# Decoder layer, feed-forward: when the finished rows of the first two blocks are stored

## The chip, the cores and the metric

The kernel runs on one core of one Trainium2 chip. The metric is the device time of one launch in microseconds (us). TensorE (PE) multiplies matrices, with its weight loads shown apart (PEld); VectorE (DVE), ScalarE (ACT) and GpSimd (POOL) work on elements; SyncE (SP) issues transfers (DMAs), which 16 DMA engines carry out. SP and POOL issue through different hardware queues, q1 and q0 in the profile.

## The reference, cut to what matters

`x` is (8, 256, 512) in float32, 2048 tokens of width 512. A layer has three parts, each followed by a residual sum and a layer norm:

```python
x = _layernorm(x + attention(x))
x = _layernorm(x + recurrence(x, ctx))
gate_w, up_w, down_w = three spline_reconstruct(...)      # 2048x512, 2048x512, 512x2048
gate, up = x @ gate_w.T, x @ up_w.T
x = _layernorm(x + (silu(gate) * up) @ down_w.T)
```

The three weights are cubic splines of few control points. The kernel uses that: it multiplies with parts of the weights exactly, and represents what is smooth by a few sums.

## The kernel before, in words

Attention and recurrence fill the first 400 us of the span; the change doesn't touch them. The feed-forward (from about 401 us) works in four blocks (`NG = 4`, loop variable `b`) of 512 tokens (`GT`), each four row tiles of 128 tokens (`TC = 4`). Everything is float32. Each engine's instructions run in the order in which the program writes them (the class `Ordered` sees to that; it is also why all lines of the profile read L308, so that tiles, not lines, tell the work apart). What isn't ready makes the engine or the queue wait, and all behind it too. A block has these steps:

1. **Inputs** (`inputs(b + 1)`, written in block b for b = 1 and 2; those of blocks 0 and 1 were made in the attention part). `tr_x2` transposes the rows of `x2`, `x2T` holds them in SBUF. They are written to a scratch tensor `xd` in device memory: four large transfers on POOL's queue, four tiny ones on SP's, three of them ahead of the block's gathers. Products `ps_mom` make moments, written to a scratch tensor `md` on POOL's queue. Then SP reads windows of `xd` (four transfers, 1408 KB) and moments from `md` (two, 640 KB) into `xg`, the operand of the next block's products. For blocks 2 and 3 these reads are kept in the list `reads` and issued by SP after the gathers of block b.
2. **Gate and up** (`gate_up(b, j)`, eight pairs). Four products `pg` and `pu`, Silu on ACT, a product on DVE into `inter`, two tiles a pair.
3. **Gathers** (`gather(b, t)`, sixteen). SP copies each `inter` tile, SBUF to SBUF, 256 KB, into every eighth partition of `nat`; eight tiles fill one `nat`, and there are two.
4. **Exact part** (`exact(b, t)`, sixteen steps of four products `y`). After the first step of block b the chains of `outcome(b - 1, t)` start (step 7).
5. **Sums** (`into_sums`, four times, after exact step 7). Products `ps_s` read `nat`: the first pair of each of the four reads all of the first `nat`, that is gathers 0 to 7, the second pair gathers 8 to 15. ACT or DVE evicts them, and POOL issues the transfer `fin<-sum` (256 KB), in this document a *fin*.
6. **Finish** (`finish`, in the last block `finish_apart`). After the last exact step the product `y<-fin` needs all four fins of the block.
7. **Outcome** (`outcome(b, t)`, a generator that a list of chains steps on). Transposes `tr_y`, residual sum and layer norm into `h3` (a tile of pool `rows`, which has 6 buffers), and as its last act the store of 128 x 512 values to `out`, 256 KB, issued by SP. It runs in the exact part of block b + 1, for the last block after `finish_apart`.

So SP's queue in blocks 1 and 2 is, in order: three small `xd` writes, 16 gathers, one small `xd` write, four window reads, two moment reads, and the four stores of the block before. Block 3 has 16 gathers, four stores of block 2 and at the end four of its own. PE's order is `tr_x`, the pairs (with `ps_mom` after the third), exact steps 0 to 7 with `tr_y` after the first, `ps_s`, exact steps 8 to 15, finish.

Of the kernel before, what the change touches and what calls it, by code (L numbers as in the profile page):

```python
# [17 lines left out]
P = 128  # L18
# [8 lines left out]
NG = NT // GT  # L27
# [288 lines left out]
def decoder_kernel(ctx: ExitStack, tc: tile.TileContext, x, xT, ctxT, wq, wkT, wvT, woT, wdownT, wup, decay, up_taps, down_taps, mom_f, sum_f, out, plan):  # L316
    nc = tc.nc
# [27 lines left out]
    nc = Ordered(tc)  # L345
    units, chains = [], []

    def slot():

        for c in list(chains):  # L350
            if next(c, c) is c:
                chains.remove(c)

    def fill(n):

        for i in range(n):
            if units:
                next(units[0][1])
                units[0][2] -= 1
                if not units[0][2]:  # L360
                    units.pop(0)
            if i % 2:
                slot()
                some_taps()

    def norm_plain(h, s, o, other=None):

        nm = small.tile([P, 1], F32, tag="nm", name="nm")
        nc.vector.tensor_scalar(nm, s, -1.0 / D, None, ALU.mult)
        yield  # L370
        ss = small.tile([P, 1], F32, tag="ss", name="ss")
        nc.scalar.activation(o if other is None else other, h, AF.Square, bias=nm, accum_out=ss)
        yield
        va = small.tile([P, 1], F32, tag="va", name="va")
        nc.gpsimd.tensor_scalar(va, ss, 1.0 / D, EPS, ALU.mult, ALU.add)
        rs = small.tile([P, 1], F32, tag="rs", name="rs")
        nc.gpsimd.tensor_tensor(rs, va, neghalf[:, 0:1], ALU.pow)
        yield
        nc.vector.tensor_scalar(o, h, nm, rs, ALU.add, ALU.mult)
# [457 lines left out]
    sf = work.tile([P, NTILE, K2], F32, name="sf", bufs=1)  # L837
    nc.sync.dma_start(out=sf, in_=sum_f)
    made[0] = -1e9
    inters, ys, sorted_, xps, nats = {}, {}, {}, {}, {}  # L840

    def gate_up(b, j):

        pgs, pus = [], []
        for w, pool, tag, to in ((wg, ps_mm, "mm", pgs), (wu, ps_big, "big", pus)):
            for h in range(2):
                at = slice(h * K2, (h + 1) * K2)
                ps = pool.tile([P, GT], F32, tag=tag, name="pg" if w is wg else "pu")
                nc.tensor.matmul(ps, lhsT=w[at, j * P : (j + 1) * P], rhs=xgs[b][at, j, :], start=True, stop=True)
                to.append(ps)  # L850
        for h in range(2):
            sg = work.tile([P, GT], F32, tag="sg", name="sg")
            nc.scalar.activation(sg, pgs[h], AF.Silu)
            inter = work.tile([P, GT], F32, tag="inter", name="inter", bufs=NTILE)
            nc.vector.tensor_tensor(inter, pus[h], sg, ALU.mult)
            inters[b, 2 * j + h] = inter

    def gather(b, t):

        g, r = t // NSUM, t % NSUM  # L860
        if not r:
            nats[b, g] = work.tile([P, NSUM, GT], F32, tag=f"nat{g}", name="nat", bufs=1)
        nc.sync.dma_start(out=nats[b, g][r::NSUM], in_=inters[b, t])

    def exact(b, t):

        if t == 0:
            ys[b] = [ps_big.tile([P, GT], F32, tag="big", name=f"y{d}") for d in range(ND)]
        for d in range(ND):
            q = slice(d * 32, (d + 1) * 32)  # L870
            nc.tensor.matmul(
                ys[b][d], lhsT=wd[q, t * P : (t + 1) * P], rhs=inters[b, t][q, :], start=(t == 0), stop=(b == NG - 1 and t == NTILE - 1)
            )

    def into_sums(b, v):

        if v == 0:
            sorted_[b] = late.tile([P, ND, GT], F32, tag="fin", name="fin")
        acc = ps_mm.tile([P, GT], F32, tag="mm", name="ps_s")
        for g in range(NTILE // NSUM):  # L880
            for a in range(2):
                u = 2 * v + a
                nc.tensor.matmul(
                    acc[a * K2 : (a + 1) * K2, :],
                    lhsT=sf[:, g * NSUM + u, :],
                    rhs=nats[b, g][:, u, :],
                    start=(g == 0),
                    stop=(g == NTILE // NSUM - 1),
                )
        o = work.tile([P, GT], F32, tag="inter", name="sum", bufs=NTILE)  # L890
        (nc.vector.tensor_copy if v % 2 else nc.scalar.copy)(o, acc)
        nc.gpsimd.dma_start(out=sorted_[b][v::ND], in_=o)
# [14 lines left out]
    def finish_apart(b):  # L907


        y = late.tile([P, ND, GT], F32, tag="ys", name="ys")  # L910
        for d in range(ND):
            (nc.vector.tensor_copy if d % 2 else nc.scalar.copy)(y[:, d, :], ys[b][d])
        ys[b] = y
        acc = [ps_mm.tile([P, GT], F32, tag="mm", name="ps_c") for _ in range(ND)]
        chain = [outcome(b, t, ps_big, "big") for t in range(TC)]
        for n, at in enumerate((slice(0, GT // 2), slice(GT // 2, GT))):
            for d in range(ND):
                nc.tensor.matmul(
                    acc[d][:, at],
                    lhsT=wd[:, (NTILE + d) * P : (NTILE + d + 1) * P],  # L920
                    rhs=sorted_[b][:, d, at],
                    start=True,
                    stop=True,
                )
                nc.vector.tensor_tensor(y[:, d, at], acc[d][:, at], y[:, d, at], ALU.add)
                if n and d == 1:
                    next(chain[0])
                    next(chain[1])
                    next(chain[0])
        next(chain[2])  # L930
        next(chain[3])
        chains.extend(chain)

    def outcome(b, t, pool=ps_mm, tag="mm"):

        tr = pool.tile([P, D], F32, tag=tag, name="tr_y")
        for d in range(ND):
            nc.tensor.transpose(tr[:, d * P : (d + 1) * P], ys[b][:, d, t * P : (t + 1) * P], ident)
        yield
        h3 = rows.tile([P, D], F32, tag="row", name="h3")  # L940
        s3 = small.tile([P, 1], F32, tag="s3", name="s3")
        nc.vector.scalar_tensor_tensor(h3, tr, 1.0, xps[b][:, t, :], ALU.mult, ALU.add, accum_out=s3)
        yield from norm_plain(h3, s3, h3, tr)
        r0 = (b * TC + t) * P
        nc.sync.dma_start(out=out[r0 : r0 + P, :], in_=h3)

    def residual(b):

        xp = late.tile([P, TC, D], F32, tag="x2p", name="x2p")
        xps[b] = xp  # L950
        i = 0
        for at, h0, n, dr, m in copies:
            for a in range(n):
                nc.gpsimd.tensor_copy(
                    xp[:, :, at + a * m : at + (a + 1) * m],
                    x2[:, b * TC : (b + 1) * TC, h0 + dr * a : h0 + dr * a + 26 * (m - 1) + 1 : 26],
                )
                i += 1
                if i % 6 == 0:
                    yield  # L960

    def settle():
        while chains:
            slot()

    for b in range(NG):
        if 0 < b < NG - 1:
            units.append(["i", inputs(b + 1), 2 * DC])
            fill(DC)
        for j in range(NTILE // 2):  # L970
            gate_up(b, j)
            gather(b, 2 * j)
            gather(b, 2 * j + 1)
            if b:
                slot()
            if b and j == 2:
                fill(DC)
        if b == 0:
            fill(2 * DC)
        while reads:  # L980
            reads.pop(0)()
        for t in range(NTILE):
            exact(b, t)
            if b and t == 0:
                chains += [outcome(b - 1, c) for c in range(TC)]
            slot()
            if b == 0 and t < 5:
                slot()
            if b == 0 and t == 4:
                settle()  # L990
                done.close()
                late = ffn["mom"] = ctx.enter_context(tc.tile_pool(name="late", bufs=1, side="right"))
            if t == 7:
                settle()
                chains.append(residual(b))
                for v in range(NSUM // 2):
                    into_sums(b, v)
        assert not units
        (finish if b + 1 < NG else finish_apart)(b)
# [53 lines left out]
```

## Time and profile before

| | us |
|---|---|
| median of three runs | 603.2 |
| the three runs | 602.25, 603.2, 605.68 |
| the profiled execution | 604.72 |
| its span, first to last instruction | 602.9 |

The difference of the last two, 1.8 us, lies around the span. In the profiled execution the granted TensorE clock averaged 0.994 of full speed. The feed-forward stretches of PE in it:

| block | pairs begin | sums `ps_s` | finish ends |
|---|---|---|---|
| 0 | 401.06 | 431.62 to 438.64 | 449.35 |
| 1 | 451.09 | 479.48 to 486.52 | 501.00 |
| 2 | 502.74 | 531.13 to 538.17 | 550.19 |
| 3 | 550.19 | 574.79 to 581.90 | 594.9 with the last `tr_y` |

How to read the profile: a line of a group gives line, engine, operation, `out<-in` by the program's tile names and the number of instructions. A chain of waits follows the work that ended last back to what released it. A windows view gives for each stretch the busy time of each engine (with its number of instructions), the granted clock, the busy share of the 16 DMA engines and what they moved in GB/s. SP's timeline shows when a transfer was issued, not when it landed; landings come from the trace's semaphore updates.

### The profile page before, as it was taken

To read this page: it belongs to the slowest core of one execution; us is meant where nothing else is said; L and a number is where in the kernel's file an instruction comes from. 1 tells how busy PE (TensorE), PEld (TensorE's weight loads), DVE (VectorE), ACT (ScalarE), POOL (GpSimd) and SP (SyncE) were. 2 spreads that over 40 slices of the span, in tenths; PEclk is the share of its full clock that TensorE was granted. 3 is DMA by queue.
4 is the path that set the end of the run, shared out by engine and by line. 5 is a ranking of instruction groups with operands and counts; after the bars stand their busy time and mean duration, and the time that the engine had idled before them with its cause. 6 is when DMAs were issued, how large, how long until landed. Compare 5 with 4: busy or idle time off the path is not lost.

```text
span 602.9 us, 9715 instructions
## 1 busy us (share of the span) xinstructions
PE 578.9 (96%) x3354; PEld 294.1 (49%) x3354; DVE 337.1 (56%) x750; ACT 277.9 (46%) x820; POOL 218.7 (36%) x495
## 2 busy tenths in 40 slices
PE   9999999998999999999999899999999989999994
PEld 4544555555455555555555555444343434433443
DVE  0203634658676665786664877766826505623716
ACT  0115644656654555664554677564315303513502
POOL 0001997165544335544340212200371261143144
PEclk9999999999999999999999999999999999999998
DMA  8104253034224115324110564669129975984941
GB/s 299 59 0 157 80 169 112 27 110 147 61 69 141 35 54 175 105 71 130 46 36 5 167 158 114 174 152 213 39 79 247 194 220 150 231 208 140 212 152 70
DMA packets 38960, 75.50 MB, mean 125 GB/s; under 512 B 3936, under 2 KB 8288, under 8 KB 38912
## 3 DMA queue, kind: packets, MB, share of 16 engines
q1 hardware_dynamic: 34576, 62.75, 39.4%
q0 software_dynamic: 3328, 10.96, 5.5%
q10 hardware_dynamic: 1008, 1.18, 0.6%
q8 instruction: 26, 0.43, 0.3%
q14 instruction: 22, 0.18, 0.1%
HBM read 42.86 MB, written 11.04 MB: 89 GB/s over the span
## 4 chain that ended last, share of the span: by engine, by line
PE 82%; DVE 9%; ACT 3%; DMA 3%; issue 2%; POOL 0%; POOLq 0%; DVEq 0%; ACTq 0%
PE y L308 10%; PE ps_k L308 9%; PE ps_v L308 9%; PE ps_o L308 8%; PE ps_q L308 7%; PE tr_e L308 7%; PE sc L308 5%; PE av L308 5%; PE pg L308 5%; PE ps_s L308 5%; PE pu L308 5%; DVE nmax L308 3%; DMA fin<-sum 3%; PE ps_mom L308 2%; ACT e L308 2%; DVE eT L308 2%
## 5 line engine op out<-in xcount | busy, mean ns | idle before, releaser
L308 ACT ACTIVATE e<-sc,nmax 128x256 f32<-128x256 f32 x256 | 120.3, 481 | 101.0 <-DVE nmax L308 100.9
L308 DVE TENSOR_REDUCE nmax<-sc 128x2 f32<-128x512 f32 x128 | 84.5, 682 | 73.6 <-PE sc L308 67.6
L308 POOL TENSOR_TENSOR taps<-taps 128x256 f32<-128x256 f32 (+1 forms) x144 | 88.9, 617 | 32.9 <-DMA taps<-in_down_taps 25.1
L308 PEld LDWEIGHTS tr_e<-ident,e 128*128 128x128 f32 x512 | 56.9, 140 | 25.2 <-issue 22.5
L308 PE MATMUL tr_e<-ident,e 128*128 128x128 f32 x512 | 68.3, 276 | 0.6 <-DVE eT L308 0.4
L308 PE MATMUL y<-inter,wd 32*128 32x512 f32 x512 | 63.0, 598 | 0.0
L308 PE MATMUL ps_o<-w_o,yT 128*128 128x512 f32 x128 | 60.0, 600 | 1.5 <-DVE eT L308 1.2
L308 PE MATMUL ps_k<-xT_g,w_k 128*128 128x512 f32 x128 | 58.7, 600 | 0.6 <-DVE eT L308 0.6
L308 PE MATMUL ps_v<-w_v,xT_g 128*128 128x512 f32 x128 | 58.6, 598 | 0.4 <-DVE eT L308 0.4
L308 PE MATMUL ps_q<-xT_g,w_q 128*128 128x512 f32 x128 | 58.2, 596 | 0.0
L308 POOL TENSOR_SCALAR va<-ss 128x1 f32<-128x1 f32 x32 | 7.3, 228 | 135.3 <-ACT x L308 85.8
L308 POOL TENSOR_TENSOR rs<-va,neghalf 128x1 f32<-128x1 f32 x48 | 28.8, 600 | 69.7 <-DVE va L308 66.9
L308 ACT ACTIVATION_READ_ACCUMULATOR e<-sc,nmax 128x1 f32 x256 | 53.3, 208 | 0.0
L308 DVE TENSOR_TENSOR inter<-pu,sg 128x512 f32<-128x512 f32 x64 | 41.3, 687 | 18.3 <-PE pu L308 9.4
L308 ACT ACTIVATE sg<-pg 128x512 f32<-128x512 f32 x64 | 37.3, 597 | 18.4 <-PE pg L308 18.4
L308 DVE COPY eT<-tr_e 128x512 f32<-128x512 f32 x64 | 43.7, 683 | 0.5 <-PE tr_e L308 0.4
L308 PEld LDWEIGHTS y<-inter,wd 32*128 32x128 f32 x512 | 26.7, 184 | 32.7 <-issue 26.9
L308 PE MATMUL av<-eT,v_g 128*32 128x256 f32 x512 | 36.7, 385 | 5.0 <-ACT eT L308 2.7
L308 ACT COPY eT<-tr_e 128x512 f32<-128x512 f32 x64 | 37.5, 586 | 2.4 <-PE tr_e L308 2.4
L308 POOL TENSOR_TENSOR r<-r 128x1024 f32<-128x1024 f32 x8 | 15.2, 1894 | 63.3 <-DMA r<-in_ctxT 63.2
L308 PE MATMUL sc<-k_g,q_g 32*128 32x256 f32 x512 | 37.4, 401 | 0.2 <-ACT e L308 0.2
L308 PEld LDWEIGHTS ps_v<-w_v,xT_g 128*128 128x128 f32 x128 | 23.1, 190 | 25.5 <-issue 24.3
(101 smaller groups left out, 742.7 us busy)
## 6 DMA issues: line engine op xcount, KB each, us to landing
nat<-inter SPq DMA_DIRECT2D x64, 256.0 KB
taps<-in_down_taps SPq DMA_DIRECT2D x40, 256.0 KB
taps<-in_up_taps SPq DMA_DIRECT2D x16, 384.0 KB
xg<-xd SPq DMA_DIRECT2D x8, 616.0 KB
r<-in_ctxT SPq DMA_DIRECT2D x8, 512.0 KB
x_t<-in_x SPq DMA_DIRECT2D x16, 256.0 KB
fin<-sum POOLq DMA_DIRECT2D x16, 256.0 KB, 5.4
out<-h SPq DMA_DIRECT2D x16, 256.0 KB
```

The source lines that it names most:

```text
L308: return lambda *a, **k: self.tc.keep_in_program_order(f(*a, **k))
```

## The change

`outcome` no longer issues its store at once when its block is 0 or 1 (`NG - 2` is 2). It puts the store in the list `stores`. The loop over the pairs takes one store from the list ahead of each pair. The list is filled in the exact part of block b + 1 and so emptied in the first four pairs of block b + 2: the stores of block 0 in block 2, those of block 1 in block 3. Blocks 2 and 3 store as before. Each of the deferred stores stands in SP's queue ahead of the two gathers of its pair.

```diff
-    inters, ys, sorted_, xps, nats = {}, {}, {}, {}, {}
+    inters, ys, sorted_, xps, nats, stores = {}, {}, {}, {}, {}, []
...
         yield from norm_plain(h3, s3, h3, tr)
         r0 = (b * TC + t) * P
-        nc.sync.dma_start(out=out[r0 : r0 + P, :], in_=h3)
+        store = lambda: nc.sync.dma_start(out=out[r0 : r0 + P, :], in_=h3)
+        if b < NG - 2:
+            stores.append(store)
+        else:
+            store()
...
         for j in range(NTILE // 2):
+            if stores:
+                stores.pop(0)()
             gate_up(b, j)
             gather(b, 2 * j)
             gather(b, 2 * j + 1)
```

## The prediction

> **What bounds the kernel now.** I read the page first, then the chain of waits stretch by stretch, because only the last third of the span is touched.
>
> ```profile
> PE 578.9 (96%) x3354; PEld 294.1 (49%) x3354; DVE 337.1 (56%) x750; ACT 277.9 (46%) x820; POOL 218.7 (36%) x495
> DMA  8104253034224115324110564669129975984941
> ```
>
> TensorE carries the time. A store never stands in a chain itself; it counts only if it delays a transfer that TensorE waits for. The DMA row reaches 9 and 8 in the feed-forward, so this can happen. Next, the chain of waits around the end of a block, for blocks 0, 1 and 2 (columns: start, length, what):
>
> ```profile
> 431.62 7.02 PE ps_s L308 x32
> 438.64 10.71 PE y L308 x72
> 449.35 1.75 PE tr_x L308 x16
> ```
> ```profile
> 487.53 8.00 DMA fin<-sum
> 495.54 0.09 issue
> 495.63 5.37 PE y L308 x8
> 501.00 1.75 PE tr_x L308 x16
> ```
> ```profile
> 539.18 7.20 DMA fin<-sum
> 546.38 0.14 issue
> 546.52 3.67 PE y L308 x8
> 550.19 1.06 PE pg L308 x4
> ```
>
> From the end of the sums (438.64, 486.52, 538.17) to the end of `finish`, block 0 needs 10.71 us, block 1 501.00 - 486.52 = 14.48, block 2 550.19 - 538.17 = 12.02. The excess, 3.77 and 1.31 us, is all that can be won; both times the last `fin<-sum` landed late. In block 1 TensorE stood for 2.05 us (timeline of PE) and its `finish` then took 5.37 instead of 3.67. The windows view says why: the clock.
>
> ```profile
> 495.00:497.00 2.00, 1.37 (x3) 0.99 0.37 140
> 497.00:499.00 2.00, 2.00 (x4) 0.50 0.01 4
> 499.00:501.00 2.00, 2.00 (x5) 0.66 0.00 0
> ```
>
> The last three columns are granted clock, DMA share and GB/s. The clock is 0.50 after the 2.05 us of idleness. After block 2's 1.29 us it stayed 1.00. So block 1's excess is some 2.05 us of waiting and 1.70 of slow clock.
>
> **Where the queue of SP stands.** Its own timeline has no barrier: an instruction leaves when its own wait is over.
>
> ```profile
> 479.05 1.65 SPq L308 DMA_DIRECT2D xg<-md  x2
> 480.80 3.24 SPq L308 DMA_DIRECT2D out<-h  x4
> 502.62 1.11 SPq L308 DMA_DIRECT2D xd<-x2T  x3
> 505.47 16.99 SPq L308 DMA_DIRECT2D nat<-inter  x16
> ```
>
> The stores stand behind block b+1's inputs (`xg`). These do not use all 16 DMA engines: while they run alone (478 to 482) the share is 0.75. By the trace's semaphore updates the four fins of block 1, issued at 482.28 to 487.53, landed at 492.56, 493.48, 494.56 and 495.54; block 3's, with no inputs before it, 2.3 us after issue. Of each fin's 16 completions five come early; the packet records show the rest only after `xg`, then about one for one with packets of the stores (41 and 46 in one us).
>
> **Taken away from blocks 1 and 2.** One fin lands per 0.99 us (2.98 / 3) in that mixture. A store behind a store lands per 0.61 us (576.08 to 577.92, three steps). A fin is four packets per engine and shares with four of a store's eight: 0.31 us. Without stores the last fin comes 4 x 0.31 = 1.24 us sooner.
> - *Block 1:* at 494.30 instead of 495.54. TensorE was through at 493.58, so 2.05 becomes 0.81 us of waiting, below the 1.29 that left the clock alone. Gain 1.24 + 1.70 = 2.94 us; bounds 0 (`xg` alone decides) and 3.77. What is late next is still fin, behind `xg`.
> - *Block 2:* three of its four stores leave. The fourth does not: block 3 has no `inputs`, so its first store stands in SP's queue right behind block 2's `xg<-md` (531.50) and leaves as before. Its eight packets fall among the fins, 0.61 us. Gain 1.24 - 0.61 = 0.63; with that one too 1.24, at most 1.31.
>
> **Put into the gathers of blocks 2 and 3.** Issuing costs SP 0.33 to 0.50 us a store; the gathers are paced by products and landings (16 in 16.99 us, 0.55 each), so SP has room. In block 2 the first store stands behind three `xd<-x2T` that wait for the transposes of block 2's start; the others stand behind gathers 2, 4 and 6, and the gathers behind them. The row buffers (6) suffice: a store's row is next wanted in the second half of its block. DVE, ACT and POOL change nothing. What counts is DMA time ahead of the gathers.
>
> ```profile
> 507.00:528.00 21.00, 21.00 (x118) 9.25 (x118) 13.74 (x30) 10.81 (x21) 3.24 (x8) 1.00 1.05 229
> 555.00:574.00 19.00, 19.00 (x120) 9.21 (x120) 13.22 (x29) 10.02 (x20) 3.29 (x8) 1.00 1.07 216
> 574.79 7.11 PE ps_s L308 x32
> ```
>
> The engines are never free here (share 1.05 and 1.07), but move only 216 to 229 GB/s; the stores behind them ran at some 400 in the slices from 574.5. So something other than the engines' time limits a gather, and a store may slip beside it. Call the delay per store x. No row shows a store amid gathers; bounds: 0 (all slips beside) and 0.61 (none). A gain below nothing is excluded, as the bytes are only added. Nearest row: when gathers begin after a pause, their packets are recorded at 147 in the first us at 84 ns each, then 100 at 166 ns; some 47 packets are taken up ahead, three quarters of the 64 that 0.61 us would hold at 100 per us. I take x = 0.2.
> - *Block 2, sums:* last gather landed 530.09, its first reader (second half of the first sum) starts about 531.97. Slack 1.9 us: 4x = 0.8 costs nothing, 2.44 costs 0.5.
> - *Block 2, fin:* the inputs stand behind the gathers on the same queue, their second half waits for a row landing behind them (SP stood until 529.87); so the fin moves by 4x = 0.8. With the 0.63 from above: a loss of 0.17, between +0.63 (x = 0) and -1.81 (x = 0.61).
> - *Block 3, sums:* last gather landed 575.48, PE's sequencer waited for it until 575.57, the reader ran at 575.67. Slack 0.1 us at most. Three stores: 3x - 0.1 = 0.5 us; bounds 0 and 1.73. The final stores are unmoved.
>
> **Sum.** -2.94 + 0.17 + 0.5 = -2.3 us against the profiled execution, 604.7 (span 602.9 and 1.8 around it): 602.4. The median shown is 603.2. The 1.70 us of slow clock may be missing there: the three runs lie 3.4 us apart, and no view tells which had it. If it is missing, only -0.6 is left of the median, 602.6; if not, 600.9. I say 601.7.
>
> **Two rules weighed.** Fin lay 8.00 us between issue and landing in block 1, 2.3 in block 3. The Trainium skill, DMA: Bandwidth & Descriptors, section Queues, rings and completion order, says that an engine takes turns between the queues it has work for, packet by packet. By that, fin would share with `xg` from the start, land after perhaps twice 2.3 us (an estimate) and be no wait before the change either; the sum would be the cost alone, +0.7 us. The packets of block 1 speak against it, and I go by the row.
> The clock fell after 2.05 us of idleness. The Trainium skill, TensorE: Matmul & The Clock Gate, Part 1, has the gate judged in free-running windows of some 3.4 us and released only after an idle window; by it 2.05 us would not be enough and the clock would cost nothing in any rival. The rows show 0.50, so it costs.
>
> **Rivals.**
> 1. *The stores are free and fin is early (x = 0, no engine lags):* both excesses go, -5.1 us of the profile, -3.4 without the clock's part: 598.1 to 599.8, say 599.4. For it: stores at 400 GB/s, gathers at 216. Against it: the share of 1.07, and the store that stays in block 2.
> 2. *A wait for gathers takes the place of the wait for fin, slower:* the stores stand in front of the gathers at their full 0.61 us. Block 3's sums lose 1.73, block 2's fin 1.81; from x = 0.35 on the wait there (1.29 - 0.63 + 4x) passes the 2.05 us that cost clock, another 1.70. At x = 0.61: -2.94 + 1.81 + 1.73 + 1.70 = +2.3 us: 605.5 from the median, 607.2 if the median had no slow clock to lose. I name 605.5. For it: one FIFO, and block 3's slack of 0.1 us. Against it: 216 GB/s.
> 3. *It does not do what it says, since `xg` alone holds fin:* block 1 keeps its 2.05 us; costs of 0.7 stay: 603.9. For it: fin moved only after `xg`. Against it: landings 0.99 us apart while the stores moved.
>
> **Chances.** Forecast 0.58 (601.7; its own range 600.0 to 602.9), rival 1 0.22, rival 2 0.12, rival 3 0.08. A measurement of this kernel tells about 0.5% from no change, 3.0 us: faster is below 600.2, slower above 606.2. Rival 1 and a few hundredths of the forecast are faster (0.25), half of rival 2 is slower (0.06), the rest is the same (0.69). The range, 599.0 to 605.6, takes in most of rivals 1 and 2 and all of rival 3.
>
> **What would show it.** Right: the piece between block 1's sums and its `finish` shrinks from 8.00 us of `fin<-sum` to under 7; no clock of 0.50 there; `finish` of block 1 takes 3.67; one store leaves right after block 2's `xg<-md`; `ps_s` of block 3 has a gap of about 0.5 us after its first four matmuls, ended by `nat<-inter`. Wrong: that gap is 0 (rival 1) or near 1.7 (rival 2); `fin<-sum` of block 2 is later against `ps_s` by a us or more (rival 2); block 1 waits as before (rival 3).

## The result, and the profile after

The median is 603.73 us (602.37 to 605.76, 14 runs) against 602.27 (601.29 to 605.68, 14 runs) before: ratio 1.0024, 95% interval 1.0012 to 1.0035. The change is slower by about 1.4 us. A gain of 1.5 us had been forecast, from 603.2 to 601.7; the sign was wrong. Two later comparisons agree: 1.0021 (1.0009 to 1.0032) for the change run again, and 1.0018 for one half of it below. One execution of each kernel, of 1188 and of 1509 us, was disturbed and is counted nowhere; the second was the profiled one of the change run again, which so has no profile to read.

The chain of waits of the changed kernel at the end of block 1 and of block 2 (start, length, what):

```profile
487.22 7.08 PE y L308 x64
494.30 0.62 issue
494.92 3.67 PE y L308 x8
498.59 1.75 PE tr_x L308 x16
```
```profile
536.78 7.92 DMA fin<-sum
544.69 0.14 issue
544.83 5.37 PE y L308 x8
550.20 1.06 PE pg L308 x4
```

Block 1 looks as hoped: no `DMA fin<-sum` in the chain, a stop of 0.62 us, and `finish` at its full-speed 3.67. But block 2 now looks as block 1 did before: the last fin takes 7.92 us, TensorE stands for 2.01 us (timeline of PE: `[2.01 <-DMA fin<-sum]`), and `finish` takes 5.37. The windows view (the last three columns are granted clock, DMA share, GB/s) has the reason:

```profile
544.00:546.00 2.00, 1.17 (x3) 0.93 0.24 71
546.00:548.00 2.00, 2.00 (x3) 0.50 0.00 0
548.00:550.00 2.00, 2.00 (x4) 0.71 0.00 0
```

In these two executions the slow clock has moved by one block. SP's timeline shows the stores where they were said to go, ahead of the gathers of block 2 and block 3, the first of block 1 still right behind block 2's `xg<-md`:

```profile
501.37 0.37 SPq L308 DMA_DIRECT2D out<-h  x1
503.06 1.36 SPq L308 DMA_DIRECT2D nat<-inter  x2
504.47 1.36 SPq L308 DMA_DIRECT2D out<-h  x1
...
530.14 1.63 SPq L308 DMA_DIRECT2D xg<-md  x2
531.87 0.43 SPq L308 DMA_DIRECT2D out<-h  x1
552.92 1.26 SPq L308 DMA_DIRECT2D nat<-inter  x2
554.23 0.59 SPq L308 DMA_DIRECT2D out<-h  x1
```

And the sums of block 3 show no gap (timeline of PE; a gap would split the line and stand in brackets behind it):

```profile
574.74 7.09 PE L308 MATMUL ps_s<-nat,sf 128*64 128x512 f32 x32
```

By this pair of profiles the two kernels are equal, 602.9 us of span each. The runs are not equal, so one of the two profiles must be a poor sample. Each run also records its mean granted clock. Of 116 executions of the kernel before in the comparisons of the experiments, one ran at 604 us or more with a mean clock of 0.994 or less. Of 24 of the changed kernel, eight did (on average 605.07 us, the other 16 603.21; the kernel before without its one 602.44). The first profile of before, 604.72 us at 0.994, was such a rare execution. (The 14 runs of before in the first comparison, whose clocks are not on record, hold one more of 604 us or more, 605.68.)

### The profile page after: what moved, and what is told of

The parts are those of the page before. It is cut to its first block, busy times and chain, and to the rows that moved or that the text cites. A ratio compares the mean times of both kernels' runs of the same rounds, so it can differ in the third digit from the quotient of the medians.

```text
span 602.9 us, 9707 instructions
## 1 busy us (share of the span) xinstructions
PE 579.3 (96%) x3354; PEld 294.1 (49%) x3354; DVE 337.2 (56%) x750; ACT 277.6 (46%) x820; POOL 219.2 (36%) x495
## 4 chain that ended last, share of the span: by engine, by line
PE 83%; DVE 10%; ACT 3%; issue 1%; DMA 1%; POOL 0%; POOLq 0%; DVEq 0%; ACTq 0%
PE y L308 11%; PE ps_k L308 9%; PE ps_v L308 9%; PE ps_o L308 8%; PE ps_q L308 7%; PE tr_e L308 7%; PE sc L308 5%; PE pg L308 5%; PE ps_s L308 5%; PE av L308 5%; PE pu L308 5%; DVE nmax L308 3%; PE ps_mom L308 2%; ACT e L308 2%; DVE eT L308 2%
## 5 line engine op out<-in xcount | busy, mean ns | idle before, releaser
L308 POOL TENSOR_TENSOR r<-r 128x1024 f32<-128x1024 f32 x8 | 15.2, 1894 | 63.8 <-DMA r<-in_ctxT 63.8
```

The source lines that it names most:

```text
L308: return lambda *a, **k: self.tc.keep_in_program_order(f(*a, **k))
```

## The experiments

Theories 1 to 3 were written before only_b0, only_b1, left_out and pool_late. Theory 1 is the prediction's own mechanism, carried on to block 2: stores hold the fins back, and block 0's, ahead of block 2's gathers, push the inputs and the fins behind them. Theory 2: the harm is block 1's first store, right behind block 2's inputs. Theory 3: the cost lies in no wait for fin. Theory 4 came after the results of these four: a fin shares the DMA engines with the reads of the inputs, not with the stores behind them ("with the clock": a low clock after block 2's wait is the rest of the cost). Theory 5 came after before_again, two_ahead, eight_ahead and moments_after: a store amid gathers alone is carried beside them for nothing. "Wait" is the idle time of TensorE ahead of `finish`, read from the one profile of each kernel; the ratio is to the kernel before, run in the same rounds, with its 95% interval.

### before_again: the kernel before, for a second profile

No edit.

> The kernel before, unchanged, for a second profile. Theory 4 (a fin shares the engines with the reads of the inputs, not with the stores behind them; the 2.05 us in block 1 of the first profile was one lagging DMA engine of that execution): block 1 waits 0.5 to 0.8 us at full clock, block 2 1.0 to 1.3 us, fins of block 1 complete on most engines 7.5 us after the sums as before, without a last engine 1.5 us later. Rival (the stores hold fin back): block 1 waits 1.8 to 2.1 us again. Ratio 1.000.

Measured: ratio 1.0001 (0.9990 to 1.0011). The timeline of PE at the end of its block 1, and at the end of its block 2:

```profile
487.69 7.15 PE L308 MATMUL y<-inter,wd 32*128 32x512 f32 x64
495.57 0.67 PE L308 MATMUL y<-fin,wd 128*128 128x512 f32 x1 [0.73 <-issue]
...
544.68 3.67 PE L308 MATMUL y<-fin,wd 128*128 128x512 f32 x8 [1.21 <-DMA fin<-sum]
```

Block 1 waits 0.73 us, not 2.05, and its clock stays at 1.00 (windows view; the last three columns are granted clock, DMA share, GB/s):

```profile
495.00:497.00 2.00, 1.43 (x4) 1.00 0.66 253
497.00:499.00 2.00, 2.00 (x6) 1.00 0.06 23
```

So there was next to nothing in block 1 for the change to win: 0.73 before, 0.62 after. The semaphore updates tell what was odd in the first profile. Counted from the end of the sums, in us:

| kernel, block 1, last fin | five engines | the next ten by | the last one |
|---|---|---|---|
| before, first profile | 3.7 to 3.9 | 7.6 | 9.1 |
| before_again | 3.8 to 4.0 | 7.8 | 7.8 |
| after | 3.8 to 3.9 | 7.5 | 7.7 |
| left_out | 3.8 to 4.0 | 7.7 | 7.8 |

In the first profile one engine of the 16 brought each of the four fins 1.4 to 1.6 us after the others. A fetch of instructions of 16 KB, 1.05 us long, is recorded on the DMA engines 3.9 us after the sums there, and 0.6 to 2.2 us after them in the other three. That fits, but the records don't say which engine carried it, so it is not shown; and it is hardly the whole cause, since in that execution the last engine is already 0.9 us behind the others with the last three gathers, which land from 476 to 479, before that fetch. Why one engine lagged stays open.

### left_out: no stores of blocks 0 and 1

```diff
-            if stores:
-                stores.pop(0)()
```

> Leaves out the stores of blocks 0 and 1 (half of the output is not written). Theory 1: block 1's wait 0.5 us, block 2's 0 to 0.3 us, no slow clock in the feed-forward; 600.0 to 600.8 us, ratio 0.996 to 0.998. Theory 3: no faster than 602.

Measured: 0.9991 (0.9982 to 1.0000), 601.96 us. The chain of waits at the end of block 1, and the timeline of PE at the end of block 2:

```profile
494.83 0.69 issue
495.53 3.67 PE y L308 x8
```
```profile
544.51 3.67 PE L308 MATMUL y<-fin,wd 128*128 128x512 f32 x8 [1.09 <-DMA fin<-sum]
```

This is the run that decides the prediction's main step. With these stores gone the waits are 0.69 and 1.09 us, within 0.04 and 0.12 us of before_again (0.73 and 1.21). The other profiles agree. In block 1 the three with four stores behind the inputs (before_again, only_b1, dup_b3) wait 0.63 to 0.73 us, the eight without any 0.55 to 0.73. In block 2 the three without any (left_out, pool_late, dup_b3) wait 0.65 to 1.09, so that a few tenths are not excluded there. Stores behind the inputs do not hold the fins back by anything near 1.24 us. The packets that go with the fins one for one are there all the same. The DMA view (queue, packets, MB, share) of five us from about 2 us after block 1's sums, first left_out, then the first profile of before:

```profile
q0 software_dynamic: 231, 0.77, 47.1%
q1 hardware_dynamic: 194, 0.37, 25.3%
```
```profile
q0 software_dynamic: 232, 0.77, 45.8%
q1 hardware_dynamic: 227, 0.43, 26.8%
```

In left_out there is nothing left on q1 but `xg`, and 194 packets are there all the same, against 227 with the stores. Theory 1 fails on its first half, the relief of blocks 1 and 2; its times of 600.0 to 600.8 are missed. Theory 3, that the cost lies in no wait for fin, is decided by the next two.

### only_b0 and only_b1: one half of the change each

```diff
-        if b < NG - 2:
+        if b == 0:
```

> Defers the stores of block 0 alone, into block 2; block 1's stay as before. Theory 1 (the jam moves: block 0's stores, ahead of block 2's gathers, push the inputs and the fins behind them): block 1 as after the change (wait for fin 0.5 us, no slow clock), block 2 carries four stores ahead and four behind, wait 2.4 to 2.8 us instead of 1.98, slow clock in most executions; 603.5 to 605.0 us, ratio 1.002 to 1.005. Theory 2 (block 1's first store, which slips out behind block 2's inputs, is the harm): block 2 waits no longer than before, 1.3 us; ratio 0.996 to 0.999. Theory 3 (the cost lies in no wait for fin): ratio as after the change, 1.002, with waits as before.

Measured: 1.0018 (1.0008 to 1.0029), 603.64 us, four of 12 runs at a clock of 0.992. Block 1 waits 0.73 us, block 2:

```profile
545.06 5.37 PE L308 MATMUL y<-fin,wd 128*128 128x512 f32 x8 [1.97 <-DMA fin<-sum]
```

```diff
-        if b < NG - 2:
+        if b == 1:
```

> Defers the stores of block 1 alone, into block 3; block 0's stay as before. Theory 1: block 1 waits as before (up to 2.05 us), block 2's wait falls from 1.29 to about 0.7 us, no gap in block 3's sums; ratio 0.998 to 1.000. Theory 2: block 2's wait stays at 1.3 us or grows; ratio 1.000 to 1.002. Theory 3: ratio 1.002 to 1.003.

Measured: 0.9998 (0.9989 to 1.0006), 602.12 us, none of 11 at a low clock. Block 1 waits 0.63 us although block 0's stores stand where they stood, block 2 1.02, and block 3's sums have no gap. Timeline of PE, block 2:

```profile
544.18 3.67 PE L308 MATMUL y<-fin,wd 128*128 128x512 f32 x8 [1.02 <-DMA fin<-sum]
```

So the cost is that of block 0's stores in block 2, as far as the intervals tell. Block 1's first store behind block 2's inputs has no part in it: only_b0 hasn't got it there and waits the same 1.97. Theories 2 and 3 fall. Theory 1 had expected a longer wait of only_b0 than of the change, 2.4 to 2.8 us, from four stores ahead and four behind. It is not longer: the four behind count for nothing, which is left_out's finding again.

### two_ahead and eight_ahead: the dose

```diff
-        if b < NG - 2:
+        if b == 0 and t < 2:
```

> Defers the first two stores of block 0 into block 2; all others as before. Theory 4 with the clock at the edge: block 2 waits some 1.5 us (1.4 to 1.7), half way between 1.1 and 2.0, slow clock in few executions; ratio 1.000 to 1.0015. Rival (each store ahead costs alike, the clock has no part): ratio 1.0012, half of that of four.

Measured: 1.0005 (0.9996 to 1.0013), no run of 11 at a low clock. The wait, 1.35 us, is below what theory 4 said; the rival's 1.0012 lies within the interval, so the ratio does not decide. Timeline of PE, block 2:

```profile
543.86 3.67 PE L308 MATMUL y<-fin,wd 128*128 128x512 f32 x8 [1.35 <-DMA fin<-sum]
```

```diff
-        if b < NG - 2:
-            stores.append(store)
+        if b == 0:
+            stores.append(store)
+            dup = ffn["dram"].tile([P, D], F32, tag="dup", name="dup", bufs=4)
+            stores.append(lambda: nc.sync.dma_start(out=dup, in_=h3))
...
-            if stores:
-                stores.pop(0)()
+            for _ in range(2):
+                if stores:
+                    stores.pop(0)()
```

> Defers the four stores of block 0 into block 2 and writes each of these tiles a second time into scratch memory beside its store: eight transfers ahead of block 2's gathers, all else as before. Theory 4 with the clock: block 2 waits 2.6 to 3.2 us and the clock is slow after it in nearly every execution; ratio 1.004 to 1.007. Rival (each store ahead costs alike, no clock): ratio 1.0036, twice that of four.

Measured: 1.0082 (1.0063 to 1.0101), 607.49 us, more than either said, since a second wait appears (timeline of PE, block 2):

```profile
528.11 1.08 PE L308 MATMUL ps_s<-nat,sf 128*64 128x512 f32 x4
531.31 6.23 PE L308 MATMUL ps_s<-nat,sf 128*64 128x512 f32 x28 [2.12 <-issue]
537.47 7.15 PE L308 MATMUL y<-inter,wd 32*128 32x512 f32 x64
546.36 3.67 PE L308 MATMUL y<-fin,wd 128*128 128x512 f32 x8 [1.73 <-DMA fin<-sum]
```

After four products of the sums, the first half, the second half waits for the last gather. Five of six runs have a low clock; the profile is of the sixth, the fastest. When the last gather of block 2 lands, against the start of the sums:

| stores ahead of block 2's gathers | last gather | wait in sums | wait for fin |
|---|---|---|---|
| 0 (before, before_again) | -0.97, -1.08 | 0 | 1.29, 1.21 |
| 2 (two_ahead) | -0.97 | 0 | 1.35 |
| 4 (only_b0, after) | 0.32, 0.40 | 0 | 1.97, 2.01 |
| 8 (eight_ahead) | 2.90 | 2.12 | 1.73 |

In these profiles the first two stores cost nothing; the next two push the gathers by 1.3 us, 0.65 each, and the four after them by 2.5, 0.63 each, near the 0.61 us of a store behind a store: up to a point free, then all of it. The 1.3 us stand clear of the scatter (seven profiles with no store ahead of block 2's gathers lie from -0.78 to -1.45, five with four of them from 0.23 to 1.51); that the first two are free rests on one profile.

### late_pairs and dup_b3: does the place matter?

```diff
-        if b < NG - 2:
+        if b == 0:
...
-            if stores:
+            if stores and j > 3:
```

> Defers the stores of block 0 alone, into the pairs 4 to 7 of block 2 instead of 0 to 3, that is behind the scratch writes of the inputs on POOL's queue. Theory 5 (a store amid gathers alone is carried beside them for nothing; what cost block 2 time was stores, scratch writes and gathers together in its first half): last gather of block 2 lands 0.5 to 1.1 us ahead of the sums as before, wait for fin 1.1 to 1.4 us; ratio 0.999 to 1.001. Rival (four stores ahead cost the same wherever they stand): last gather 0.3 to 0.6 us after the start of the sums, wait 1.9 to 2.2 us; ratio 1.001 to 1.003.

Measured: 1.0013 (1.0004 to 1.0021). The last gather lands 1.25 us after the start of the sums, later than with the stores in front; the sums wait 0.31 us, fin 1.50 (timeline of PE, block 2):

```profile
530.04 6.23 PE L308 MATMUL ps_s<-nat,sf 128*64 128x512 f32 x28 [0.31 <-DMA nat<-inter]
...
544.85 3.67 PE L308 MATMUL y<-fin,wd 128*128 128x512 f32 x8 [1.50 <-DMA fin<-sum]
```

```diff
-        if b < NG - 2:
-            stores.append(store)
+        if b == 1:
+            stores.append(store)
+            dup = ffn["dram"].tile([P, D], F32, tag="dup", name="dup", bufs=4)
+            stores.append(lambda: nc.sync.dma_start(out=dup, in_=h3))
...
-            if stores:
-                stores.pop(0)()
+            for _ in range(2):
+                if stores and j:
+                    stores.pop(0)()
```

> Defers the stores of block 1 alone, into pairs 1 to 4 of block 3, and writes each of these tiles a second time into scratch memory: eight transfers amid block 3's gathers, none in block 2's fins. Theory 5: all are carried beside the gathers, a gap of at most 0.5 us in the sums of block 3; ratio 0.999 to 1.001. Rival (a few stores are free, each further one costs the 0.6 us that separate eight from four in block 2): a gap of 2.5 to 3.5 us in block 3's sums; ratio 1.004 to 1.006.

Measured: 1.0074 (1.0060 to 1.0087). Timeline of PE, block 3:

```profile
572.15 1.08 PE L308 MATMUL ps_s<-nat,sf 128*64 128x512 f32 x4
576.33 7.92 PE L308 MATMUL ps_s<-nat,sf 128*64 128x512 f32 x28 [3.10 <-DMA out<-h]
```

A gap of 3.10 us, as the rival said, and a low clock in five of six runs. Theory 5 fails twice: a store is not carried beside the gathers for nothing. Three in block 3 (after) are free, eight cost some 3.3 us of gathers (last landing 3.94 us after the start of the sums against 0.55 and 0.75 before); four late ones in block 2 cost 2.2 together. What makes the first two or three free is left open. With the stores among the gathers, q1 moves up to 336 GB/s in single us of block 3's first half (after), against some 205 behind it; but gathers and stores both have packets of 2 KB there, so the records don't say which of them went faster, and no run shows why late stores cost more.

### pool_late: the stores where the DMA engines are idle

```diff
-            if stores:
-                stores.pop(0)()
...
-        store = lambda: nc.sync.dma_start(out=out[r0 : r0 + P, :], in_=h3)
+        queue = nc.gpsimd if b < NG - 2 else nc.sync
+        store = lambda: queue.dma_start(out=out[r0 : r0 + P, :], in_=h3)
...
         (finish if b + 1 < NG else finish_apart)(b)
+        while stores:
+            stores.pop(0)()
```

> Issues the stores of blocks 0 and 1 on POOL's queue after finish of blocks 1 and 2, where the DMA engines were idle for 5 us or more and POOL is through with its copies. Theory 1: as with the stores left out, plus at most 0.4 us if block 2's scratch writes wait for them: 600.2 to 601.2 us, ratio 0.997 to 0.999. Theory 3: no faster than 602.

Measured: 0.9998 (0.9987 to 1.0009), one of 12 runs at a low clock; waits 0.55 and 0.82 us. A better place than the change's, and still no gain. There is little to be had from stores: left_out, without them, gains 0.5 us in the mean of the ratio, and its interval reaches 1.0000.

### moments_after, and both: what fin does share with

```diff
-            nc.sync.dma_start(out=xg[to : to + 20], in_=from_)
+            queue.dma_start(out=xg[to : to + 20], in_=from_)
...
-                    reads.append(lambda: moments(md, xg))
+                    late_reads.append(lambda: moments(md, xg, nc.gpsimd))
...
                 for v in range(NSUM // 2):
                     into_sums(b, v)
+                while late_reads:
+                    late_reads.pop(0)()
```

> The kernel before, with the two reads of the moments (xg<-md) of blocks 2 and 3 issued on POOL's queue right behind the four fins instead of on SP's queue ahead of them; no store moves. Theory 4: fin no longer shares with the moments: block 1 waits 0 to 0.2 us, block 2 0 to 0.6 us; ratio 0.996 to 0.998. Rival (the stores hold fin back, or the window reads do): block 2's wait stays at 1.0 us or more; ratio 0.9995 to 1.001.

Measured: 0.9990 (0.9981 to 0.9999), 601.99 us. Timeline of PE at the ends of blocks 1 and 2:

```profile
494.18 2.38 PE L308 MATMUL y<-fin,wd 128*128 128x512 f32 x5 [0.15 <-issue]
...
542.32 3.67 PE L308 MATMUL y<-fin,wd 128*128 128x512 f32 x8 [0.24 <-DMA fin<-sum]
```

With the reads of the moments behind the fins the waits all but vanish, 0.73 to 0.15 and 1.21 to 0.24, with every store where it was. This is the work that the prediction had taken for the stores. It also tells how stores ahead of the gathers reach the fins: they push the gathers, these the reads of the inputs behind them on SP's queue. Against the start of block 2's sums the second read of the moments lands at 14.9 us in before_again and at 17.3 in after, the last fin at 15.2 and 16.0. The runs gain 0.6 us in the mean of the ratio, at most 1.1 by the interval, where the profile loses 1.55 us of waits; the rest is not accounted for, except that the profile is of the fastest of its 11 runs (600.77 us). It is the only version that beats both kernels beyond its interval.

`both` is the change with this edit added.

> The change, and with it the two reads of the moments of blocks 2 and 3 on POOL's queue behind the fins. Theory 4: with the moments gone from in front of the fins the change loses its cost: no wait for fin over 0.6 us, no slow clock in the feed-forward; ratio 0.998 to 1.000, that of the moments moved alone. Rival (the stores ahead cost by another way than the wait for fin): ratio 1.001 to 1.003.

Measured: 0.9993 (0.9985 to 1.0002), 601.63 us, no run at a low clock: the change's cost is gone. The waits in its profile are not what theory 4 said, 0.78 us in block 2's sums and 1.10 for fin:

```profile
529.63 6.23 PE L308 MATMUL ps_s<-nat,sf 128*64 128x512 f32 x28 [0.78 <-DMA xg<-xd]
535.79 7.15 PE L308 MATMUL y<-inter,wd 32*128 32x512 f32 x64
544.04 3.67 PE L308 MATMUL y<-fin,wd 128*128 128x512 f32 x8 [1.10 <-DMA fin<-sum]
```

The wait for fin is again that of one late engine: 15 had completed the last fin 14.2 us after the start of the sums, the sixteenth did so at 16.1, and TensorE was through with the exact part at 15.2. So the ratio bears theory 4 out, and the profile does so in part.

### keep_warm, keep_warm_half and after_again: the clock's share

```diff
+        if b == NG - 2:
+            warm = ps_mm.tile([P, GT], F32, tag="mm", name="ps_warm")
+            for _ in range(4):
+                nc.tensor.matmul(warm, lhsT=ident, rhs=inters[b, NTILE - 1], start=True, stop=True)
         (finish if b + 1 < NG else finish_apart)(b)
```

> The change, and in block 2 four more products of 128 x 512 between the last exact step and finish, into a PSUM tile that nobody reads: 1.7 us of work in the 2.0 us in which TensorE waits for fin. Theory 4 with the clock: no execution has the slow clock after block 2 (none at a mean clock of 0.992), the slower cluster of runs at 604.0 to 605.8 is gone and the faster one at 602.4 to 603.9 stays; ratio 1.0005 to 1.0018. Rival (the slower executions have another cause than the clock after this wait): two clusters again, ratio 1.002 to 1.003.

Measured: 1.0059 (1.0046 to 1.0073), 605.95 us. The four products took 3.63 us, twice what was written, so they outlast the wait by 1.6 us; over the 603.2 us of the change without the low clock that makes 604.8, and another 1.1 us is not accounted for. No run had a low clock, but this kernel does not tell the causes apart. `keep_warm_half` has `range(2)` in place of `range(4)`:

> As keep_warm with two products instead of four. The four took 3.63 us, twice what was said, and more than the wait; two are 1.8 us in a wait of 2.0. Theory 4 with the clock: no run at a mean clock of 0.992, the cluster at 604.0 us and above is gone, the one at 602.4 to 603.9 stays, finish of block 2 takes 3.7 us; ratio 1.0005 to 1.0018. Rival (the slower executions have another cause, or products for nothing cost by themselves as the 606 us of keep_warm may say): ratio 1.002 or more.

Measured: 1.0017 (1.0005 to 1.0028), median 603.00 us; `finish` follows the filling at once and takes 3.67. One of 11 runs is at a low clock (606.27 us), the others lie at 602.4 to 604.1.

> The change, unchanged, on the same chip and in the same rounds as keep_warm_half. Theory 4 with the clock: block 1 waits 0.6 to 0.7 us and block 2 1.8 to 2.1 us; a third to a half of the runs at a mean clock of 0.992 and 604 us or more; ratio 1.0015 to 1.0030.

Measured: 1.0021 (1.0009 to 1.0032); two of 10 runs at a low clock, 604.72 and 605.83 us, fewer than was said; its waits are not on record. One of 11 in keep_warm_half against eight of 24 points the way of the clock, but is too few to show it. What the counts do show, over all runs: the low clock comes with about 1.9 us (605.07 against 603.21), near the 1.70 by which `finish` lengthens.

## Why the prediction was wrong, point by point

- **"A fin is four packets per engine and shares with four of a store's eight: 0.31 us. Without stores the last fin comes 4 x 0.31 = 1.24 us sooner."** This step failed. The 2 KB packets beside the fins belonged to `xg<-md`, not to `out<-h`: both queue up on q1, and the records give a queue and a size, not a tile. left_out measured 0.04 us in block 1 and 0.12 in block 2 instead of 1.24 (against before_again). The landings in the trace of before would have told it: the second `xg<-md` lands on its ten engines from 493.28 to 494.79, amid the fins, and the first store on ten of its engines only from 494.33 to 495.92.
- **"Gain 1.24 + 1.70 = 2.94 us" in block 1.** It measured 0.1 (0.73 to 0.62 us). The 2.05 us and the slow clock were those of one execution: of 116 others one was as slow at so low a clock. The prediction had seen that the runs lay 3.4 us apart and the profile high among them, and still made its main term from a single profile.
- **Block 2: "+0.63 (x = 0) and -1.81 (x = 0.61)", taken as a loss of 0.17.** The mechanism of the cost was right, stores ahead of gathers push inputs and fins behind them. The wait went from 1.21 to 2.01, a loss of 0.8: just the 4x = 0.8 of the sum, but there was no 0.63 to win against it. That the 0.8 fits is in part luck. x is not one number (0 for the first two stores, 0.65 for the next two, 1.4 us in all), and of these 1.4 us only 0.8 reached the last fin.
- **"from x = 0.35 on the wait there ... passes the 2.05 us that cost clock, another 1.70."** At 1.97 to 2.01 us the clock falls in about a third of the executions (12 of 36 of the change and only_b0), at 1.2 in none to speak of. The length of the stop alone doesn't set it, but how much of it falls into one stretch of 3.413 us (last section). 8 of 24 times 1.9 us are 0.6 us a run.
- **Block 3: "3x - 0.1 = 0.5 us".** No gap at all; the three stores of after are free there.
- **The sum.** 0.8 us of wait and 0.6 of clock make 1.4 us lost; 1.46 were measured between the medians, and 0.77 between the executions without a low clock (603.21 and 602.44), which is the wait alone. The prediction had 2.94 gained against 0.67 lost.
- **Rivals.** Rival 3 (`xg` alone holds fin) was right for what the change was to win, and given 0.08; rival 2 was right in kind for what it cost, with a smaller price. They are no alternatives: both held, and their sum is the result. That rival 3's 603.9 lies near the 603.73 is luck: 0.5 of its costs of 0.7 stood in block 3's sums, where there was none, and it started from 603.2, which the comparison has at 602.27.
- **The rule on queues.** The Trainium skill, DMA: Bandwidth & Descriptors, section Queues, rings and completion order, was set aside for the row. It holds between fins and moments, which alternate on the engines (40 and 43 packets in the us from 490, first profile). But no fin moved beside the window reads on the engines that carried these: the first fin, issued at 482.28, completed on the last eleven engines from 489.72 on, after these reads had landed there, 487.22 to 488.71. There the row differs from the rule, if a packet is one record.

## What to carry to other kernels

Before a transfer is blamed for a wait, name it by its landing, not by its queue and packet size, and look at what is left when it is taken out: one run with the stores left out would have settled this case. A wait to be won must be seen in more than one execution; a profile that lies above the median of its own runs is a sample of the bad case. And a transfer moved to an earlier point of a queue is a debt to everything behind it there: here four stores pushed the gathers by 1.4 us, and two stages later the wait grew by 0.8.

## What the runs showed of the hardware

- A stop of TensorE of about 2.0 us costs more or nothing by chance, and the clock records of the 15 profiles (all but that of after_again) tell by which. Every stretch at full clock is a whole number of 3.413 us long (590.506 us is 173 times that, 539.306 158 times, 47.787 14 times), and the slow stretch within the feed-forward, in the four profiles that have one (before, after, only_b0, dup_b3), is one such piece. Counted off in these pieces, 19 at full clock are followed by the half clock (four in the feed-forward, the others at the end of the span), and TensorE was idle for 1.92 us or more in each of them; in the other 2574 it was idle for 1.79 or less. The stops of 2.05 (before), 2.01 (after) and 1.97 us (only_b0) lay whole in one piece. That of 2.12 us in eight_ahead was cut by a boundary into 1.79 and 0.33 and cost no clock. Where a stop falls differs from run to run: one of 2.0 us would be caught in about half of the placements, an estimate from these numbers; 12 of 36 runs were.
- The Trainium skill, TensorE: Matmul & The Clock Gate, Part 1, has a free-running window of this length, which agrees with these pieces; that a whole idle window would be needed does not agree with the 1.92 us.
- A fin completes on five engines some 3 us after its issue and on the other eleven only when they are through with the window reads, up to 9.2 us after (blocks 1 and 2 of before_again, after and left_out; 10.3 on the late engine of the first profile).
- The time of a transfer of 256 KB is that of its slowest engine: one late engine of 16 put some 1.5 us on each of four fins (first profile).
